# A term of the second layer moved into a PSUM group, and row sums moved from VectorE to ScalarE, in a four-layer graph kernel

## Chip, cores and metric

One core of one Trainium2 chip. The metric is the device time of one execution in microseconds (us). Each kernel is compared with the kernel before on the same chip, in the same rounds. A ratio is the mean time of one kernel's fast runs over that of the other's of the same rounds, so it is not quite the ratio of the medians that I quote; the bracket behind it is its 95% interval. Lower is better.

## The reference

Four graph layers over one 4096 x 4096 weighted adjacency matrix `adj` (f32) and 4096 nodes of 128 features. Each layer is added to its input and normalised. The change touches three of its lines, one in the second layer and two in the last:

```python
# second layer: two Chebyshev convolutions (K = 3)
out = Tx0 @ W[0] + Tx1 @ W[1] + (2.0 * (L @ Tx1) - Tx0) @ W[2] + b     # Tx1 = L @ Tx0, L = adj
# third layer: attention with 4 heads of 32; tau_sum sums over the sources
tau = adj_t * exp(max(0.2 * C, C));  z = (adj_t * tau / tau_sum) @ h_prime
# last layer: mean over the neighbours
deg = clip(sum(adj, axis=1), 1.0);   out = h @ W_self + (adj @ h / deg) @ W_neigh
```

## The kernel before

The second layer makes three products with the adjacency matrix, each as eight blocks of 512 columns, 32 matmuls (4096 rows in tiles of 128) into one PSUM bank per block; each matmul leaves two records in the trace. PSUM is the memory that TensorE adds its products up in; a group is a run of matmuls that add into one bank, and the copy that takes the sum out is called its evacuation. A chunk is the piece of `adj` that a load brings. In what follows "product one" multiplies x, "product two" t1 = adj x, "product three" v = 2 h W2. Product one also sums the degrees, which only the last layer needs:

```python
def propagate(stationary, order=range(NB), look=None):
    for ib in range(NB):
        p = ps_acc.tile([P, IB], F32, name="pacc")
        for n, c in enumerate(order):
            a = chunk(ld, adjT, ib, c)
            if look: look(a, n == 0)
            for k in range(TB):
                nc.tensor.matmul(p, stationary(c * TB + k), a[:, k, :], start=..., stop=...)
        yield ib, slice(ib * IB, (ib + 1) * IB), p

def degree(a, first_one):                       # product one, VectorE, per chunk
    s = l1h.tile([P, 2, IB], F32, name="dhalf")
    nc.vector.tensor_add(s, a[:, 0:2, :], a[:, 2:4, :])
    ...                                         # two more additions into dsum

for ib, blk, p in propagate(lambda jt: x[:, jt, :], finished, degree):
    nc.scalar.copy(t1T[:, blk], p)
    pd = ps_mm.tile([P, TB], F32, name="pmm")
    for k in range(TB):
        nc.tensor.matmul(pd[:, k:k + 1], dsum[:, k * P:(k + 1) * P], ones, start=True, stop=True)
    nc.vector.tensor_scalar_max(rdeg[:, ib * TB:(ib + 1) * TB], pd, 1.0)
    q = transpose4(ps_tr, "ptr", ...)
# ... product two ...
for ib, blk, p in propagate(lambda jt: v[:, jt, :]):            # product three
    nc.scalar.copy(lvT, p)
    for k in range(TB):
        nc.tensor.matmul(q[:, k, :], lvT[...], ident, start=True, stop=False)
        for hh in range(HH):
            nc.tensor.matmul(q[:, k, :], hT[:, hh, ...], W1B[:, HH + hh, :], start=False, stop=...)
    # then ph = h (W0 - W2), two matmuls of 512 columns
```

The third layer runs in eight passes, (mp, hp): four blocks of 1024 columns, two pairs of heads. A pass walks over 32 row tiles. For each, ScalarE squares 704 columns of the chunk, VectorE makes `tau` and part of `tau2`, GpSimd the rest, TensorE sums `den` and `num`. At the end of a pass ScalarE evacuates the sums:

```python
    sq = l2w.tile([P, OWN], F32, name="sq", bufs=2)
    nc.scalar.activation(sq, a[:, 0:OWN], AF.Square)
    ...
# end of a pass
nd = l2w.tile([P, 2, IB], F32, name="nd")
nc.scalar.copy(nd[:, 1, :], den)
nc.scalar.copy(nd[:, 0, :], num)
q = transpose4(ps_x, "px", lambda k: nd[:, 1, k * P:(k + 1) * P])
```

The order of the instructions on each engine is not that of the source: it is chosen at build time, within what the buffers and the data allow.

Of the kernel before, what the change touches and what calls it, by code (L numbers as in the profile page):

```python
# [10 lines left out]
F32 = mybir.dt.float32  # L11
BF16 = mybir.dt.bfloat16
# [20 lines left out]
def adj_resnorm_d4(ctx: ExitStack, tc: tile.TileContext, x_in, xT_in, adj, adjT, w0g, w0gT, a0, w1a, b1a,  # L33
# [53 lines left out]
    mv = const.tile([P, NT, 2], F32, name="mv")  # L87
    es = const.tile([P, NT, H], F32, name="es")
    cs = const.tile([P, NT, H], F32, name="cs")
    flag = const.tile([1, 1], I32, name="flag")  # L90

    def chunk(pool, src, ib, c):
# [318 lines left out]
    def network(usual):  # L411

        with ExitStack() as whole:
# [4 lines left out]
            with ExitStack() as first, ExitStack() as l1h_pool:  # L418
                ps_acc, ps_tr, ps_mm = [first.enter_context(tc.tile_pool(name=n, bufs=2, space=PSUM, reuse_waits="tile"))
                                        for n in ("ps_acc", "ps_tr", "ps_mm")]  # L420
                if not usual:
                    layer0_general(ps_acc, ps_tr, ps_mm)
                    finished = list(range(NB))
                ld = enter(name="ld", bufs=6)
                if usual:
                    finished = layer0(ld, ps_acc, ps_tr, ps_mm)
                dv = state.tile([96, N], BF16, name="dv")
                selD = state.tile([96, H, P], BF16, name="selD")
                l1 = l1_pools.enter_context(tc.tile_pool(name="l1", bufs=1, reuse_waits="tile"))
                l1w = l1_pools.enter_context(tc.tile_pool(name="l1w", bufs=2, reuse_waits="tile"))  # L430
                l1h = l1h_pool.enter_context(tc.tile_pool(name="l1h", bufs=1, reuse_waits="tile"))
                W1A = l1h.tile([P, 3, HID], F32, name="W1A")
                nc.scalar.dma_start(W1A, w1a.rearrange("k p f -> p k f"))
                W1B = l1h.tile([P, 3 * HH, F], F32, name="W1B")
                nc.scalar.dma_start(W1B, w1b.rearrange("k (h p) f -> p (k h) f", p=P))

                def elu(dst, p, bias):
                    r = l1w.tile([P, IB], F32, name="elu_r")
                    n = l1w.tile([P, IB], F32, name="elu_n")
                    nc.scalar.activation(r, p, AF.Relu, bias=bias)  # L440
                    nc.vector.tensor_scalar(n, p, bias, 0.0, op0=ALU.add, op1=ALU.min)
                    nc.scalar.activation(n, n, AF.Exp)
                    nc.vector.scalar_tensor_tensor(dst, n, -1.0, r, op0=ALU.add, op1=ALU.add)

                def propagate(stationary, order=range(NB), look=None):


                    for ib in range(NB):
                        p = ps_acc.tile([P, IB], F32, name="pacc")
                        for n, c in enumerate(order):  # L450
                            a = chunk(ld, adjT, ib, c)
                            if look:
                                look(a, n == 0)
                            for k in range(TB):
                                nc.tensor.matmul(p, stationary(c * TB + k), a[:, k, :], start=n == 0 and k == 0,  # L455
                                                 stop=n == NB - 1 and k == TB - 1)
                        yield ib, slice(ib * IB, (ib + 1) * IB), p

                t1 = state.tile([P, NT, F], F32, name="t1", tag="yn")
                t1T = l1.tile([P, N], F32, name="t1T", tag="t1T")  # L460
                hT = l1h.tile([P, HH, N], F32, name="hT")
                wd = l1h.tile([P, HH, F], F32, name="wd")
                nc.vector.tensor_sub(wd, W1B[:, 0:HH, :], W1B[:, 2 * HH:3 * HH, :])
                w2x = l1h.tile([P, HH, F], F32, name="w2x")
                nc.vector.tensor_scalar_mul(w2x, W1B[:, 2 * HH:3 * HH, :], 2.0)
                dsum = l1h.tile([P, IB], F32, name="dsum")

                def degree(a, first_one):

                    s = l1h.tile([P, 2, IB], F32, name="dhalf")  # L470
                    nc.vector.tensor_add(s, a[:, 0:2, :], a[:, 2:4, :])
                    if first_one:
                        nc.vector.tensor_add(dsum, s[:, 0, :], s[:, 1, :])
                    else:
                        nc.vector.tensor_add(dsum, dsum, s[:, 0, :])
                        nc.vector.tensor_add(dsum, dsum, s[:, 1, :])


                for ib, blk, p in propagate(lambda jt: x[:, jt, :], finished, degree):
                    nc.scalar.copy(t1T[:, blk], p)  # L480
                    pd = ps_mm.tile([P, TB], F32, name="pmm")
                    for k in range(TB):
                        nc.tensor.matmul(pd[:, k:k + 1], dsum[:, k * P:(k + 1) * P], ones, start=True, stop=True)
                    nc.vector.tensor_scalar_max(rdeg[:, ib * TB:(ib + 1) * TB], pd, 1.0)
                    q = transpose4(ps_tr, "ptr", lambda k: t1T[:, (ib * TB + k) * P:(ib * TB + k + 1) * P])
                    nc.vector.tensor_copy(t1[:, ib * TB:(ib + 1) * TB, :], q)
                nc.vector.reciprocal(rdeg, rdeg)

                v = state.tile([P, NT, F], F32, name="v")
                for ib, blk, p in propagate(lambda jt: t1[:, jt, :]):  # L490
                    t2T = l1w.tile([P, IB], F32, name="t2T")
                    nc.vector.scalar_tensor_tensor(t2T, p, 2.0, xT[:, blk], op0=ALU.mult, op1=ALU.subtract)
                    for hh in range(HH):
                        ph = ps_mm.tile([P, IB], F32, name="pmm")
                        for k, r in enumerate((xT[:, blk], t1T[:, blk], t2T)):
                            nc.tensor.matmul(ph, W1A[:, k, hh * P:(hh + 1) * P], r, start=k == 0, stop=k == 2)  # L496
                        elu(hT[:, hh, blk], ph, B1A[:, hh:hh + 1])
                    q = ps_tr.tile([P, TB, F], F32, name="ptr")
                    for k in range(TB):
                        for hh in range(HH):  # L500
                            nc.tensor.matmul(q[:, k, :], hT[:, hh, (ib * TB + k) * P:(ib * TB + k + 1) * P],
                                             w2x[:, hh, :], start=hh == 0, stop=hh == HH - 1)
                    nc.vector.tensor_copy(v[:, ib * TB:(ib + 1) * TB, :], q)


                w = state.tile([P, NT, F], F32, name="w", tag="yn")
                h0T = l1.tile([P, N], F32, name="h0T", tag="t1T")
                for ib, blk, p in propagate(lambda jt: v[:, jt, :]):
                    lvT = l1w.tile([P, IB], F32, name="t2T")
                    nc.scalar.copy(lvT, p)  # L510
                    q = ps_tr.tile([P, TB, F], F32, name="ptr")
                    for k in range(TB):
                        nc.tensor.matmul(q[:, k, :], lvT[:, k * P:(k + 1) * P], ident, start=True, stop=False)
                        for hh in range(HH):
                            nc.tensor.matmul(q[:, k, :], hT[:, hh, (ib * TB + k) * P:(ib * TB + k + 1) * P],  # L515
                                             W1B[:, HH + hh, :], start=False, stop=hh == HH - 1)
                    nc.vector.tensor_copy(w[:, ib * TB:(ib + 1) * TB, :], q)  # L517
                    ph = ps_mm.tile([P, IB], F32, name="pmm")
                    for hh in range(HH):
                        nc.tensor.matmul(ph, wd[:, hh, :], hT[:, hh, blk], start=hh == 0, stop=hh == HH - 1)  # L520
                    nc.scalar.copy(h0T[:, blk], ph)
# [68 lines left out]
            def attention(l2w, bufs, mp, hp):  # L590
# [20 lines left out]
                for nt in range(NT):  # L611
# [4 lines left out]
                    a = a2t[:, nt % 2, :]  # L616
                    sq = l2w.tile([P, OWN], F32, name="sq", bufs=2)
                    nc.scalar.activation(sq, a[:, 0:OWN], AF.Square)  # L618
                    tau = l2w.tile([P, 2, WB], F32, name="tau", bufs=bufs)
                    tau2 = l2w.tile([P, 2, WB], F32, name="tau2", bufs=bufs)  # L620
                    E = lambda h: es[:, nt, 2 * hp + h:2 * hp + h + 1]
# [112 lines left out]
            for mp in range(NW):  # L734
                for hp in range(H // 2):
                    if (mp, hp) != (0, 0):
                        for _ in attention(l2w, 3, mp, hp):
                            next(pieces, None)
                for _ in pieces:
                    pass  # L740
                for j in (2 * mp, 2 * mp + 1):
# [35 lines left out]
```

## Time and profile before

| | before |
|---|---|
| time, median of 3 | 2380.44 us (2375.94 to 2380.57) |
| profiled span | 2376.4 us |
| layer one | 371.7 |
| products one, two, three | 233.4, 274.0, 257.8 |
| last product of layer two with attention pass (0,0) | 347.1 |
| the other seven passes | 108.7, 129.0, 108.2, 119.9, 110.4, 118.4, 110.4 |
| from the last evacuation to the end | 87.3 |

The rows add up to the span. A pass is read as the time from one evacuation of `den` to the next; the seven are (0,1), (1,0), (1,1), (2,0), (2,1), (3,0), (3,1).

### The profile page before, as it was taken

To read this page: it belongs to the slowest core of one execution; us is meant where nothing else is said; L and a number is where in the kernel's file an instruction comes from. 1 tells how busy PE (TensorE), PEld (TensorE's weight loads), DVE (VectorE), ACT (ScalarE), POOL (GpSimd) and SP (SyncE) were. 2 spreads that over 40 slices of the span, in tenths; PEclk is the share of its full clock that TensorE was granted. 3 is DMA by queue.
4 is the path that set the end of the run, shared out by engine and by line. 5 is a ranking of instruction groups with operands and counts; after the bars stand their busy time and mean duration, and the time that the engine had idled before them with its cause. 6 is when DMAs were issued, how large, how long until landed. Compare 5 with 4: busy or idle time off the path is not lost.

```text
span 2376.4 us, 23290 instructions
## 1 busy us (share of the span) xinstructions
PE 2247.5 (95%) x8798; PEld 860.8 (36%) x8798; DVE 1371.0 (58%) x1981; ACT 484.2 (20%) x716; POOL 847.5 (36%) x541
## 2 busy tenths in 40 slices
PE   5899999999999999999999998879998999999988
PEld 3334444444444444444433332112222222222233
DVE  4443458777110110000156656999799999999965
ACT  5665000000000000000122121223222222322220
POOL 0000000000000000000043424999698899889950
PEclk8899999999999999999999998999999999999999
DMA  9988888999878778888877774446665666666655
GB/s 363 347 274 263 246 246 263 290 294 291 263 243 264 233 233 261 280 263 258 262 256 235 266 265 160 146 156 229 213 213 195 209 216 231 212 217 229 220 193 188
DMA packets 261802, 575.39 MB, mean 242 GB/s; under 512 B 9776, under 2 KB 15920, under 8 KB 261680
## 3 DMA queue, kind: packets, MB, share of 16 engines
q1 hardware_dynamic: 252352, 566.27, 73.3%
q10 hardware_dynamic: 9328, 7.54, 1.0%
q8 instruction: 71, 1.16, 0.2%
q14 instruction: 51, 0.42, 0.1%
HBM read 571.67 MB, written 2.10 MB: 241 GB/s over the span
## 4 chain that ended last, share of the span: by engine, by line
PE 83%; DVE 9%; DMA 4%; issue 2%; ACT 1%; POOL 1%; DVEq 0%; ACTq 0%; POOLq 0%
PE pacc L455 27%; PE pacc L319 10%; PE den L607 10%; PE pp L677 10%; PE pp L712 10%; PE num L607 7%; DVE tau L623 5%; DMA chunk<-in_adjT 3%; PE pmm L496 2%; PE num L677 1%; PE px L103 1%; PE pden L305 1%; DVE tau L624 1%; PE ptr L314 1%; PE px L663 1%
## 5 line engine op out<-in xcount | busy, mean ns | idle before, releaser
L623 DVE SCALAR_TENSOR_TENSOR tau<-d,es,chunk 128x1024 f32<-128x1024 f32 x512 | 634.9, 1277 | 25.1 <-issue 16.2
L627 POOL TENSOR_TENSOR tau<-tau,chunk 128x1024 f32<-128x1024 f32 x256 | 611.4, 2388 | 54.8 <-DVE tau L623 47.1
L607 PE MATMUL den<-tau,cs 128*32 128x512 f32 x2048 | 457.5, 605 | 8.6 <-DVE tau L623 8.1
L585 POOL TENSOR_TENSOR x<-x,B2R 128x512 f32<-128x512 f32 x8 | 10.1, 1268 | 1245.1 <-PE px L103 1245.1
L607 PE MATMUL num<-tau,hc 128*32 128x512 f32 x2048 | 413.8, 601 | 32.1 <-POOL tau L627 27.6
L618 ACT ACTIVATE sq<-chunk 128x704 f32<-128x704 f32 x256 | 201.5, 791 | 605.6 <-DVE tau L624 528.9
L626 POOL TENSOR_TENSOR tau<-tau,chunk 128x320 f32<-128x320 f32 x256 | 226.0, 883 | 115.7 <-PE num L607 46.9
L319 PE MATMUL pacc<-chunk,hw 128*128 128x512 f32 x512 | 254.8, 635 | 3.0 <-DVE hw L352 3.0
L677 PE MATMUL pp<-chunk,xT 128*128 128x512 f32 x448 | 243.5, 637 | 11.8 <-DMA chunk<-in_adjT 11.4
L624 DVE SCALAR_TENSOR_TENSOR tau<-d,es,sq 128x704 f32<-128x704 f32 x256 | 241.8, 944 | 18.9 <-PE num L607 14.1
L712 PE MATMUL pp<-chunk,w 128*128 128x512 f32 x512 | 235.6, 602 | 1.2 <-DVE t2T L718 1.2
L455 PE MATMUL pacc<-chunk,x 128*128 128x512 f32 x512 | 223.6, 594 | 0.0
L455 PE MATMUL pacc<-chunk,t 128*128 128x512 f32 x512 | 223.6, 592 | 0.0
L455 PE MATMUL pacc<-chunk,v 128*128 128x512 f32 x512 | 221.4, 592 | 0.0
L607 PEld LDWEIGHTS num<-tau,hc 128*32 128x32 f32 x2048 | 82.2, 109 | 248.2 <-POOL tau L627 83.5
L607 PEld LDWEIGHTS den<-tau,cs 128*32 128x32 f32 x2048 | 86.0, 108 | 222.3 <-issue 106.0
L299 DVE TENSOR_SCALAR pos<-chunk 128x2048 bf16<-128x2048 f32 x92 | 110.8, 1222 | 75.4 <-DMA chunk<-in_adjT 69.6
L517 DVE COPY w<-ptr 128x512 f32<-128x512 f32 x8 | 5.5, 692 | 246.1 <-PE ptr L515 246.1
L455 PEld LDWEIGHTS pacc<-chunk,v 128*128 128x128 f32 x512 | 97.1, 190 | 121.5 <-issue 121.5
L455 PEld LDWEIGHTS pacc<-chunk,t 128*128 128x128 f32 x512 | 96.1, 190 | 114.8 <-issue 114.8
L712 PEld LDWEIGHTS pp<-chunk,w 128*128 128x128 f32 x512 | 92.2, 190 | 124.6 <-issue 117.7
L455 PEld LDWEIGHTS pacc<-chunk,x 128*128 128x128 f32 x512 | 95.8, 190 | 113.4 <-issue 113.4
(171 smaller groups left out, 1461.1 us busy)
## 6 DMA issues: line engine op xcount, KB each, us to landing
chunk<-in_adjT SPq DMA_DIRECT2D x412, 1024.0 KB, 5.5
chunk<-in_adj SPq DMA_DIRECT2D x128, 1024.0 KB, 5.3
xT<-in_xT ACTq DMA_DIRECT2D x8, 256.0 KB, 6.6
out<-o ACTq DMA_DIRECT2D x8, 256.0 KB, 3.6
W1A<-in_w1a ACTq DMA_DIRECT2D x1, 384.0 KB, 3.5
W1B<-in_w1b ACTq DMA_DIRECT2D x1, 384.0 KB, 4.4
W0T<-in_w0gT ACTq DMA_DIRECT2D x1, 64.0 KB, 4.0
W<-in_w0g ACTq DMA_DIRECT2D x1, 64.0 KB, 6.5
```

The costliest lines, as they stand in the source:

```text
L299: nc.vector.tensor_scalar(pos, a, 0.0, None, op0=ALU.is_gt)
L319: nc.tensor.matmul(p, hw[:, j * TB + k, :], a[:, k, :], start=first and k == 0, stop=last and k == TB - 1)
L455: nc.tensor.matmul(p, stationary(c * TB + k), a[:, k, :], start=n == 0 and k == 0, stop=n == NB - 1 and k == TB - 1)
L496: nc.tensor.matmul(ph, W1A[:, k, hh * P:(hh + 1) * P], r, start=k == 0, stop=k == 2)
L607: nc.tensor.matmul(acc[q:q + 32, :], weights(nt, 2 * hp + h, is_den), r[:, h, mb * IB:(mb + 1) * IB], start=nt == 0, stop=nt == NT - 1)
L618: nc.scalar.activation(sq, a[:, 0:OWN], AF.Square)
L623: nc.vector.scalar_tensor_tensor(tau[:, h, :], D[h], E(h), a, op0=ALU.max, op1=ALU.mult)
L624: nc.vector.scalar_tensor_tensor(tau2[:, 0, 0:OWN], D[0][:, 0:OWN], E(0), sq, op0=ALU.max, op1=ALU.mult)
L626: nc.gpsimd.tensor_tensor(tau2[:, 0, OWN:WB], tau[:, 0, OWN:WB], a[:, OWN:WB], ALU.mult)
L627: nc.gpsimd.tensor_tensor(tau2[:, 1, :], tau[:, 1, :], a, ALU.mult)
L677: nc.tensor.matmul(p, y[:, (2 * mp + c) * TB + k, :], a[:, k, :], start=c == 0 and k == 0, stop=c == 1 and k == TB - 1)
L712: nc.tensor.matmul(p, w[:, c * TB + k, :], a[:, k, :], start=c == 0 and k == 0, stop=c == NB - 1 and k == TB - 1)
```

## The change

The intent: take the degree sums off VectorE and TensorE in product one, where TensorE is the bound, and let ScalarE, which has room, take them from the chunks that the third layer loads anyway; and let the term h W1 ride in the open PSUM group of product three in wide matmuls, so that what follows is a plain transpose.

```diff
-                def propagate(stationary, order=range(NB), look=None):
+                def propagate(stationary, order=range(NB), beside=None):
 ...
+                            if beside and n == 0:
+                                beside(p, ib)
 ... (function degree, dsum, the eight blocks' degree matmuls and clips: removed)
+                def times_w1(p, ib):
+                    for hh in range(HH):
+                        nc.tensor.matmul(p, W1B[:, HH + hh, :], hT[:, hh, ib * IB:(ib + 1) * IB], start=False, stop=False)
+                for ib, blk, p in propagate(lambda jt: v[:, jt, :], beside=times_w1):
 ...
-                    for k in range(TB):
-                        nc.tensor.matmul(q[:, k, :], lvT[...], ident, start=True, stop=False)
-                        for hh in range(HH): nc.tensor.matmul(q[:, k, :], hT[...], W1B[:, HH + hh, :], ...)
+                    q = transpose4(ps_tr, "ptr", lambda k: lvT[:, k * P:(k + 1) * P])
 ...                                             # attention, right behind the square
+                    if hp == 0:
+                        junk = l2w.tile([P, WB], BF16, name="junk")
+                        nc.scalar.activation(junk, a, AF.Copy, accum_out=deg[:, nt, mp:mp + 1])
 ...                                             # before the last two layer-three blocks
+                    nc.vector.tensor_reduce(rdeg, deg, AX.X, ALU.add)      # then max 1.0, reciprocal
```

More of the change, by code (lines that the diff above doesn't have):

```diff
@@ L89, in adj_resnorm_d4 @@
     cs = const.tile([P, NT, H], F32, name="cs")
+    deg = const.tile([P, NT, NW], F32, name="deg")
     flag = const.tile([1, 1], I32, name="flag")
@@ L451, in propagate @@
                             a = chunk(ld, adjT, ib, c)
-                            if look:
-                                look(a, n == 0)
                             for k in range(TB):
@@ L465, in network @@
                 nc.vector.tensor_scalar_mul(w2x, W1B[:, 2 * HH:3 * HH, :], 2.0)
-                dsum = l1h.tile([P, IB], F32, name="dsum")
-                def degree(a, first_one):
-                    s = l1h.tile([P, 2, IB], F32, name="dhalf")
-                    nc.vector.tensor_add(s, a[:, 0:2, :], a[:, 2:4, :])
-                    if first_one:
-                        nc.vector.tensor_add(dsum, s[:, 0, :], s[:, 1, :])
-                    else:
-                        nc.vector.tensor_add(dsum, dsum, s[:, 0, :])
-                        nc.vector.tensor_add(dsum, dsum, s[:, 1, :])
-                for ib, blk, p in propagate(lambda jt: x[:, jt, :], finished, degree):
+                for ib, blk, p in propagate(lambda jt: x[:, jt, :], finished):
                     nc.scalar.copy(t1T[:, blk], p)
-                    pd = ps_mm.tile([P, TB], F32, name="pmm")
-                    for k in range(TB):
-                        nc.tensor.matmul(pd[:, k:k + 1], dsum[:, k * P:(k + 1) * P], ones, start=True, stop=True)
-                    nc.vector.tensor_scalar_max(rdeg[:, ib * TB:(ib + 1) * TB], pd, 1.0)
                     q = transpose4(ps_tr, "ptr", lambda k: t1T[:, (ib * TB + k) * P:(ib * TB + k + 1) * P])
                     nc.vector.tensor_copy(t1[:, ib * TB:(ib + 1) * TB, :], q)
-                nc.vector.reciprocal(rdeg, rdeg)
                 v = state.tile([P, NT, F], F32, name="v")
@@ L507, in network @@
                 h0T = l1.tile([P, N], F32, name="h0T", tag="t1T")
-                for ib, blk, p in propagate(lambda jt: v[:, jt, :]):
+                def times_w1(p, ib):
+                    for hh in range(HH):
+                        nc.tensor.matmul(p, W1B[:, HH + hh, :], hT[:, hh, ib * IB:(ib + 1) * IB], start=False, stop=False)
+                for ib, blk, p in propagate(lambda jt: v[:, jt, :], beside=times_w1):
                     lvT = l1w.tile([P, IB], F32, name="t2T")
                     nc.scalar.copy(lvT, p)
-                    q = ps_tr.tile([P, TB, F], F32, name="ptr")
-                    for k in range(TB):
-                        nc.tensor.matmul(q[:, k, :], lvT[:, k * P:(k + 1) * P], ident, start=True, stop=False)
-                        for hh in range(HH):
-                            nc.tensor.matmul(q[:, k, :], hT[:, hh, (ib * TB + k) * P:(ib * TB + k + 1) * P],
-                                             W1B[:, HH + hh, :], start=False, stop=hh == HH - 1)
+                    q = transpose4(ps_tr, "ptr", lambda k: lvT[:, k * P:(k + 1) * P])
                     nc.vector.tensor_copy(w[:, ib * TB:(ib + 1) * TB, :], q)
@@ L738, in network @@
                             next(pieces, None)
+                if mp == NW - 1:
+                    nc.vector.tensor_reduce(rdeg, deg, AX.X, ALU.add)
+                    nc.vector.tensor_scalar_max(rdeg, rdeg, 1.0)
+                    nc.vector.reciprocal(rdeg, rdeg)
                 for _ in pieces:
```

## The prediction

> **What bounds the kernel now.** I read the page first, then the chain of work that ended last, then the busy time of each engine in windows cut at the stage borders, then the lines and timelines of the parts that the change touches.
>
> ```profile
> PE 2247.5 (95%) x8798; PEld 860.8 (36%) x8798; DVE 1371.0 (58%) x1981; ACT 484.2 (20%) x716; POOL 847.5 (36%) x541
> ...
> PE 83%; DVE 9%; DMA 4%; issue 2%; ACT 1%; POOL 1%; DVEq 0%; ACTq 0%; POOLq 0%
> ```
>
> TensorE is busy 95% of the span and is 83% of the chain; ScalarE is busy 20% and is 1% of the chain. By these two lines work taken from TensorE counts, work taken from VectorE hardly does, and ScalarE has room. An average over stages can mislead, so the stages:
>
> ```profile
> core 0: us, PE busy (x) PEld busy (x) DVE busy (x) ACT busy (x) POOL busy (x), PEclk, DMA share, GB/s
> 371.80:606.70 234.90, 233.95 (x631) 110.01 (x632) 174.25 (x254) 6.27 (x12) 0.00 (x0) 1.00 0.92 290
> ...
> 909.00:1137.00 228.00, 228.00 (x674) 111.97 (x673) 5.54 (x8) 8.37 (x15) 0.00 (x0) 1.00 0.84 264
> ...
> 1961.00:2073.00 112.00, 106.25 (x588) 26.63 (x587) 108.96 (x123) 28.86 (x41) 103.23 (x66) 1.00 0.65 226
> 2073.00:2190.00 117.00, 115.70 (x617) 31.80 (x616) 110.44 (x105) 30.91 (x48) 105.27 (x68) 1.00 0.64 216
> ```
>
> 371.8 to 606.7 is the second layer's first product, where the degrees are summed now; 909 to 1137 most of its third product. In both TensorE is busy for the whole window, but for 0.95 us in the first. VectorE's 174 us beside it lie under TensorE. The last two windows are the third layer's attention, one pass of 32 row tiles each (2073 to 2190 is one that will get the degree sums, 1961 to 2073 one that will not). There VectorE, TensorE and GpSimd are all nearly full, and ScalarE is at a quarter. So the saving, if any, is in the first two stages and the risk in the attention.
>
> What stands between the products now:
>
> ```profile
> 402.65 1.05 PE L483 MATMUL pmm<-ones,dsum 128*128 128x1 f32 x8 [0.95 <-DVE dsum L476]
> 403.56 1.10 PE L455 MATMUL pacc<-chunk,x 128*128 128x512 f32 x2
> 404.50 0.60 PE L103 MATMUL ptr<-ident,t1T 128*128 128x128 f32 x4
> 404.94 7.46 PE L455 MATMUL pacc<-chunk,x 128*128 128x512 f32 x17
> ```
>
> This is TensorE's timeline at the end of the first of eight blocks of product one. The eight records of the degree matmuls hold it from 402.65 to 403.56, after 0.95 us of waiting for VectorE's sum. The four transposes take some 0.43 us.
>
> ```profile
> 433.90 26.61 PE pacc L455 x62
> 462.70 26.61 PE pacc L455 x62
> ...
> 944.96 27.47 PE pacc L455 x64
> 976.97 27.47 PE pacc L455 x64
> ```
>
> From the chain of waits in order of time: blocks of the first product follow each other every 28.80 us, those of the third every 32.01 us. A record of a full product matmul takes 26.61/62 = 0.429 us, and each matmul leaves two.
>
> **What the Trainium skill says.** (1) "TensorE: Matmul & The Clock Gate", Back-to-back issue gap, gives N/2.4 + 2.5 ns for one isolated warm matmul, 216 ns for N=512. The trace has 0.858 us for a matmul here (f32, two records), four times that; I use the trace. (2) "ScalarE: Activation LUTs", What ACT_TABLE_LOAD costs: 186 ns + 0.833 ns per element for an ACTIVATE without pointer operands, 1039 ns at N=1024. The trace's nearest is the summing pass of layer one, 1913 ns for 2048 elements (the formula gives 1892), so it agrees within 2%, but it is followed by a read of the accumulator of 191 ns, which counts too. (3) Table sets on that page says that copy is in every set as filler; so the new copies should load no table, and the built programs do have equally many loads. No run shows it yet. (4) "PSUM — Partial Sum Buffer", The four PSUM rules: a matmul without the first flag adds where the bit is set, so two more matmuls inside an open group need no extra wait or evacuation. The trace agrees so far as the 64 records of a group run at 0.429 us each with no idle time.
>
> **The change part by part.** The built programs differ by these counts, half of each being in a fallback branch that does not run: 32 one-column matmuls less; 64 matmuls of 128 columns (W1B under hT) replaced by 16 of 512 columns; 32 products with the identity become transposes; 184 additions and 8 clips less on VectorE; 128 summing copies more on ScalarE; three small VectorE operations more.
>
> 1. First product. Per block the degree matmuls cost 403.56 - 402.65 = 0.91 us, so 8 x 0.91 = 7.3 us, plus the one wait of 0.95 us: 8.2 us, all on the path. The new period should be 64 x 0.429 + 0.43 = 27.9 us.
>
> 2. Third product. The period of 32.01 us less 64 x 0.429 = 27.47 leaves 4.54. Four records of the wd product are 4 x 0.429 = 1.72, which leaves 2.82 for the 24 records of the old mix of identity and W1B (8 + 16), 0.1175 each. After: two wide matmuls are four records, 1.72 us, and four transposes, one record each, 0.43 (as in the first product) to 0.58 (as in the last layer's): 2.15 to 2.30. Gain 0.52 to 0.67 per block, 4.2 to 5.4 in eight. The arithmetic of the W1 term is the same before and after; the gain is only that narrow f32 matmuls are dear (0.1175 us for 128 columns against 0.107 for a quarter of a wide one) and that a transpose is one record instead of two.
>
> 3. VectorE, first product:
>
> ```profile
> L471 DVE TENSOR_TENSOR dhalf<-chunk 128x1024 f32<-128x1024 f32 x64 | 78.4, 1224 | 2.0
> ...
> L476 DVE TENSOR_TENSOR dsum<-dsum,dhalf 128x512 f32<-128x512 f32 x56 | 38.7, 692 | 1.8
> L475 DVE TENSOR_TENSOR dsum<-dsum,dhalf 128x512 f32<-128x512 f32 x56 | 38.7, 691 | 1.6
> ```
>
> With 5.5 us of first additions 161 us of VectorE go, 93% of its work in that window. Beyond the 0.95 us they are worth nothing, since TensorE had no other wait on them.
>
> 4. ScalarE, attention. A summing copy of 1024 is 1913 - 1024 x 0.833 = 1060 ns, with the read 1.25 us; 128 of them are 160 us, 40 in each of the four passes over the first pair of heads. ScalarE goes from 31 to some 71 of 117 us: it does not become the bound by its sum. The squares (L618, 791 ns) are what VectorE needs from it, and they run two row tiles ahead, since they have two buffers.
>
> 5. End: three operations on 128x32 values, under 1 us (an estimate from the 353 ns of the reciprocal of that size), in the 2.5 us in which VectorE waits for the denominators' transposes before L639. Nothing.
>
> Sum on TensorE: 8.2 + 4.8 = 13 us.
>
> **Where ScalarE can give it back.** ScalarE runs in program order, so a copy whose chunk has not landed holds the squares behind it. In the comparison of the two orders the copies come in pairs ahead of squares of earlier tiles: in the third pass for instance the copies of tiles 26 and 27 stand before the square of tile 23. I took each chunk's landing from the trace of before, added 2.5 us for the pair and 0.8 us for the square, and compared with the time at which VectorE started on that square. Of 128 copies nearly all leave 0.5 to 10 us; the worst are -0.8 us in pass (1,0), -1.8 in (2,0), and -1.7 and -1.9 before and in (3,0). So some 6 us in all if each is paid in full, and the later part of a pass may not pay since a delay already there covers the next. One place shows what it looks like:
>
> ```profile
> 1649.99 0.59 ACT L684 COPY acc<-pp 128x512 f32<-128x512 f32 x1 [7.98 <-PE pp L677]
> 1650.48 1.47 ACT L618 ACTIVATE sq<-chunk 128x704 f32<-128x704 f32 x2
> 1651.31 0.95 DVE L624 SCALAR_TENSOR_TENSOR tau<-d,es,sq 128x704 f32<-128x704 f32 x1 [1.25 <-ACT sq L618]
> ```
>
> ScalarE waited 8 us for a product, two squares were late, and VectorE lost 1.25 us. Pass (1,0) has four such places. I take 5 us for ScalarE in all.
>
> **The rivals.** (a) ScalarE costs nothing: the copies fall into its idle time (its squares sat 495 us waiting for VectorE in the attention). For it: the busy sums and most of the margins. Then 2378 - 13 = 2365. (b) ScalarE's order becomes the wait: margins of 0.5 to 3 us go too, since chunks land later as passes shift, and the layer-three blocks' short chain of ScalarE copies gets copies of 1.25 us ahead of them. For it: only 4 chunks or so stand between landing and use in the later passes. That would give back 10 to 18 us: 2375 to 2383, a wash. (c) The relief of VectorE frees chunks earlier and the loads start earlier. DMA is at 0.92 of its time in that window, but TensorE has no wait on a load there: nothing. (d) The first product was bound by VectorE at block ends oftener than once; then the gain would be over 8.2 us. Against it: the idle time before the degree matmuls is 0.95 us in all.
>
> **Range and chances.** The three times lie from 2375.9 to 2380.6, so I start from 2378 rather than the median. 2378 - 13 + 5 = 2370. Rival (a) is the low side, (b) the high side, with some 4 us for the changed order in the attention on each side: 2361 to 2381. Faster by over 2% (under 2333) would need 47 us, more than three times what TensorE loses of work: 0.01. Slower by over 2% (over 2428) would need ScalarE to cost 60 us, some half microsecond in each of the 128 tiles: 0.02. Within 2%: 0.97.
>
> **What would show it.** Right: blocks of product one every 27.9 us, of product three every 31.3 to 31.5 us, TensorE without idle time in both; 128 summing copies of 1.06 us with a read of 0.19 us each; 20 table loads as now; attention passes over the first heads longer by 0 to 3 us each, with VectorE's waits for the squares up from 2.7 us to 5 or 8. Wrong: the third product's period staying near 32 (wide matmuls or transposes dearer than taken); the passes with copies longer by over 5 us, with ScalarE waiting for chunks in front of the copies (rival b); or passes shorter than now, which nothing here explains.

## The result, and the profile after

The changed kernel is correct and takes 2375.57 us (median of 4, 2370.89 to 2377.05) against 2379.89 us (median of 4): ratio 0.9982 [0.9964, 1.0]. It lies in the range that was predicted and in "within 2%", but the forecast gain of some 8 to 10 us came out as 4.3, with an interval that just reaches no gain. In five further rounds the same kernel gave 2374.3 us and 0.9977 [0.9965, 0.999]. Some 5 us of 13 are left.

The changed kernel's page, busy time and chain:

```profile
PE 2241.0 (94%) x8606; PEld 841.0 (35%) x8606; DVE 1209.7 (51%) x1791; ACT 618.9 (26%) x972; POOL 847.5 (36%) x541
...
PE 82%; DVE 8%; DMA 5%; issue 2%; ACT 2%; POOL 1%; DVEq 0%; ACTq 0%; POOLq 0%
```

VectorE lost 161 us of work and ScalarE gained 135, and the end hardly moved: neither was the bound. ScalarE's share of the chain rose from 1% to 2% and that of DMA from 4% to 5%, which is a first hint. The chain in order of time (start us, us, what), in products one and three:

```profile
430.94 27.47 PE pacc L454 x64
...
458.88 11.16 PE pacc L454 x26
...
907.78 1.72 PE pacc L495 x4
909.49 24.03 PE pacc L454 x56
933.52 0.86 PE pmm L504 x2
934.38 0.47 PE ptr L104 x4
...
939.15 1.72 PE pacc L495 x4
```

Product one's blocks now follow every 458.88 - 430.94 = 27.94 us (28.80 before), product three's every 939.15 - 907.78 = 31.37 us (32.01 before). The two wide W1 matmuls are four records and 1.72 us, the four transposes 0.47 us. Both gains came as worked out: the ledger has product one at 225.8 (-7.6) and product three at 253.3 (-4.5). The loss is in the attention. The seven passes took 819.7 us against 805.0 in this execution, 14.7 more, and 814.0 in the profiled execution of the second batch, 9.0 more.

What stands there is read best at the end of pass (2,1). ScalarE's timeline of the kernel before at that place (in brackets: idle before, and what ended it):

```profile
2056.71 0.79 ACT L618 ACTIVATE sq<-chunk 128x704 f32<-128x704 f32 x1 [3.01 <-DVE tau L624]
2060.30 0.59 ACT L635 COPY nd<-den 128x512 f32<-128x512 f32 x1 [2.80 <-PE den L607]
```

ScalarE waits for `den` and evacuates it at once. The same place in the changed kernel:

```profile
2041.47 1.46 ACT L602 ACTIVATE sq<-chunk 128x704 f32<-128x704 f32 x2
2049.08 1.06 ACT L605 ACTIVATE junk<-chunk 128x1024 bf16<-128x1024 f32 x1 [6.15 <-DMA chunk<-in_adj]
...
2051.32 0.77 ACT L602 ACTIVATE sq<-chunk 128x704 f32<-128x704 f32 x1
2051.99 1.04 ACT L605 ACTIVATE junk<-chunk 128x1024 bf16<-128x1024 f32 x1
...
2053.16 1.06 ACT L605 ACTIVATE junk<-chunk 128x1024 bf16<-128x1024 f32 x1
...
2054.89 0.56 ACT L622 COPY nd<-den 128x512 f32<-128x512 f32 x1
```

ScalarE stands 6.15 us in front of a summing copy of the *next* pass, because its chunk has not landed. Behind it in ScalarE's order are the squares of this pass and the evacuation of `den`. TensorE, changed kernel:

```profile
2051.84 0.60 PE L581 MATMUL d<-dv,selD 96*128 96x512 bf16 x2
2055.51 0.69 PE L104 MATMUL px<-ident,nd 128*128 128x128 f32 x2 [3.06 <-ACT nd L622]
```

TensorE's last records of `den` end at 2051.92 (a group of six from 2050.47, 1.45 us), so the evacuation came about 3 us late and TensorE waited 3.06 us for it. In those 3 us ScalarE was not waiting: it made the last two of four summing copies, and a square, that had piled up behind the late chunk. Six copies of the next pass stand ahead of the evacuation at the ends of (0,1) and (1,1) as well; there their chunks landed early enough, and the evacuation begins within 0.1 us of the last `den` record, as in the kernel before. Behind the wait TensorE's granted clock fell (the share of its full clock that the profile shows as granted); the windows of the changed kernel (columns as in the prediction's table; the granted clock is the third figure from the right):

```profile
2050.00:2055.00 5.00, 2.45 (x18) 0.50 (x14) 3.46 (x4) 4.94 (x11) 3.20 (x3) 0.96 0.89 306
2055.00:2058.00 3.00, 2.49 (x11) 0.50 (x11) 0.00 (x0) 1.15 (x2) 2.29 (x1) 0.50 0.79 307
2058.00:2061.00 3.00, 2.48 (x16) 1.49 (x16) 1.68 (x3) 1.63 (x3) 0.06 (x1) 0.50 0.00 0
...
2065.00:2070.00 5.00, 4.17 (x17) 1.55 (x18) 5.00 (x7) 3.64 (x10) 3.23 (x2) 1.00 0.00 0
```

For about ten microseconds TensorE ran at half clock. It is tempting to add that to the cost, but degonly, a kernel told of below, has the same order of instructions from pass (2,0) on and much the same wait, with the clock at 1.00 behind it:

```profile
2059.86 0.44 PE L104 MATMUL px<-ident,nd 128*128 128x128 f32 x2 [3.29 <-ACT nd L623]
```

```profile
2055.00:2060.00 5.00, 1.71 (x11) 0.38 (x8) 2.74 (x3) 4.97 (x10) 3.01 (x2) 1.00 0.86 275
2060.00:2065.00 5.00, 3.86 (x30) 1.23 (x34) 3.00 (x4) 2.32 (x5) 3.15 (x3) 1.00 0.37 150
```

Its clock fell only behind a later wait, at 2068 us and for about 3 us. Its passes (2,1) and (3,0) took 113.5 and 121.7 us, the changed kernel's 113.3 and 121.7. So the longer stretch of half clock cost nothing here that the passes show. The Trainium skill, "TensorE: Matmul & The Clock Gate", What's actually happening, says that the clock gate halves the array's clock after an idle window of about 3.4 us, with a window that runs freely. The traces agree only in part: 3.06 us of waiting were followed by 0.50 here, and 3.29 us in degonly were not.

### The profile page after: what moved, and what is told of

It reads as the page before. It is cut to its first block, busy times and chain, and to the rows that moved or that the text cites. A ratio compares the mean times of both kernels' runs of the same rounds, so it can differ in the third digit from the quotient of the medians.

```text
span 2375.2 us, 22876 instructions
## 1 busy us (share of the span) xinstructions
PE 2241.0 (94%) x8606; PEld 841.0 (35%) x8606; DVE 1209.7 (51%) x1791; ACT 618.9 (26%) x972; POOL 847.5 (36%) x541
## 3 DMA queue, kind: packets, MB, share of 16 engines
q8 instruction: 69, 1.13, 0.2%
## 4 chain that ended last, share of the span: by engine, by line
PE 82%; DVE 8%; DMA 5%; issue 2%; ACT 2%; POOL 1%; DVEq 0%; ACTq 0%; POOLq 0%
PE pacc L454 28%; PE pacc L320 10%; PE pp L699 10%; PE pp L664 9%; PE den L591 9%; PE num L591 7%; DVE tau L610 5%; DMA chunk<-in_adjT 3%; PE pmm L480 2%; PE px L104 1%; PE num L664 1%; DVE tau L611 1%; PE pden L306 1%; DMA chunk<-in_adj 1%; PE px L650 1%
## 5 line engine op out<-in xcount | busy, mean ns | idle before, releaser
L591 PE MATMUL den<-tau,cs 128*32 128x512 f32 x2048 | 464.3, 609 | 11.9 <-DVE tau L610 11.5
L591 PE MATMUL num<-tau,hc 128*32 128x512 f32 x2048 | 420.0, 605 | 33.5 <-POOL tau L614 26.8
L569 POOL TENSOR_TENSOR x<-x,B2R 128x512 f32<-128x512 f32 x8 | 10.1, 1267 | 1228.4 <-PE px L104 1228.4
L605 ACT ACTIVATE junk<-chunk 128x1024 bf16<-128x1024 f32 x128 | 134.9, 1054 | 111.0 <-DMA chunk<-in_adj 105.2
L454 PEld LDWEIGHTS pacc<-chunk,v 128*128 128x128 f32 x512 | 97.3, 190 | 121.9 <-issue 121.9
```

Of the source, the lines that this page charges most:

```text
L591: nc.tensor.matmul(acc[q:q + 32, :], weights(nt, 2 * hp + h, is_den), r[:, h, mb * IB:(mb + 1) * IB], start=nt == 0, stop=nt == NT - 1)
L605: nc.scalar.activation(junk, a, AF.Copy, accum_out=deg[:, nt, mp:mp + 1])
```

## The experiments

Ten kernels were run, all with five rounds. Theory A: the built order put most of the copies 2 to 8 row tiles ahead of the squares, and a copy whose chunk has not landed holds the squares and evacuations behind it. Rival B: ScalarE's 160 us (the sum of the copies' and reads' records; since records overlap, its busy time rose by 135) themselves are too much, wherever they stand; B': they are too dense in the passes that have them.

**nocopy: no degree work at all (result wrong, relative error 0.207).**

```diff
-                    if hp == 0: junk = ...; nc.scalar.activation(junk, a, AF.Copy, accum_out=...)
-                    nc.vector.tensor_reduce(rdeg, deg, AX.X, ALU.add) ...
+                    nc.vector.memset(rdeg, 0.125)
```

> The change with no degree work at all (rdeg is a constant, so the result is wrong on purpose). Its TensorE order from layer two's last product on is that of the kernel before, in every pass. All theories: the two products gain what they gained in the changed kernel, 8.1 + 4.6 = 12.7 us, so -12.7 us against before (-11 to -14). If it gains less than 9 us, the loss of the attention passes is not due to the copies at all.

Measured: 2367.87 us, 0.9952 [0.9938, 0.9966]; seven passes 804.5. Without the copies the passes are those of before. So the whole loss comes with the copies, and some 6.5 us are there to be had beyond the changed kernel's 2374.3.

**bound: the same copies, each right behind its own square.** The copy writes behind the square in one tile, so a copy cannot be ordered ahead of the squares before it. Correct. In the built program all 128 copies follow their own square, where the changed kernel has them up to 8 tiles ahead.

```diff
-                    sq = l2w.tile([P, OWN], F32, name="sq", bufs=2)
+                    sqj = l2w.tile([P, OWN + WB // 2], F32, name="sq", bufs=2)
+                    sq = sqj[:, 0:OWN]
-                        junk = l2w.tile([P, WB], BF16, name="junk")
+                        junk = sqj[:, OWN:OWN + WB // 2].bitcast(BF16)
```

> The whole change, but each summing copy writes its unused output into the same double buffer as its tile's square, so that it can't be ordered ahead of that square: in the built program each copy stands right behind its own square. The result is right. Theory A (the copies are ordered 2 to 8 tiles ahead of the squares, ScalarE then waits for chunks that have not landed and holds the squares and evacuations behind them): the 14.8 us given back in the passes from (1,0) on come back but for 0 to 3 us, so -10 to -13 us against before, ScalarE's waits of copies for chunks under 10 us (97.7 in the changed kernel). Rival B (the 160 us of ScalarE time themselves delay squares and evacuations, wherever they stand): it still gives back 10 to 15 us, so +2 to -3 us against before.

Measured: 2368.11 us, 0.9953 [0.994, 0.9966], as fast as having no copies. ScalarE does the same work in another order (the build moved some instructions of TensorE and VectorE too, see "What stays open"). Bound, ScalarE, end of pass (2,1):

```profile
2047.36 0.79 ACT L603 ACTIVATE sq<-chunk 128x704 f32<-128x704 f32 x1 [3.02 <-DVE tau L612]
2048.06 1.04 ACT L606 ACTIVATE sq<-chunk 128x1024 bf16<-128x1024 f32 x1
...
2050.95 0.58 ACT L623 COPY nd<-den 128x512 f32<-128x512 f32 x1 [1.76 <-PE den L591]
```

The evacuation again waits for `den`, not for a chunk (the second line is the summing copy, under the name of the shared tile). This is what theory A says of the pass end, and no copy waited for a chunk any more. But the seven passes still took 812.3 us in the profiled execution, 7.3 over before where 0 to 3 were forecast; 5.1 of these are in passes (1,0) and (1,1), of which more below.

**short: copies of 64 columns at the changed kernel's places (wrong, relative error 0.652).**

```diff
-                        nc.scalar.activation(junk, a, AF.Copy, accum_out=...)         # junk [P, WB]
+                        nc.scalar.activation(junk, a[:, 0:64], AF.Copy, accum_out=...) # junk [P, 64]
```

> The whole change, but each summing copy reads only 64 of the 1024 columns (wrong result on purpose), in the same places of ScalarE's order as in the changed kernel: the same waits for chunks, a quarter of the time. Theory A: the waits for chunks stay (60 to 100 us) and most of the loss with them, so 5 to 11 us given back of the 12.7, -2 to -8 us against before. Rival B: the loss goes with the length of the copies, -11 to -13 us.

Measured: 2368.8 us, 0.9952 [0.9938, 0.9966]; seven passes 812.4. ScalarE's order is nearly unchanged, each copy is short, and most of the loss of time is gone: 10.7 us under before by the medians, near what rival B forecast (-11 to -13 us) and not theory A (-2 to -8). So the place alone is not the whole cause either; place and length together are. The end of pass (2,1) shows how:

```profile
2045.73 0.26 ACT L605 ACTIVATE junk<-chunk 128x64 bf16<-128x64 f32 x1 [7.05 <-DMA chunk<-in_adj]
...
2049.61 0.56 ACT L622 COPY nd<-den 128x512 f32<-128x512 f32 x1
```

ScalarE waits as long for the same chunk, but reaches the evacuation 3.9 us after it landed, where the changed kernel needs 5.8; TensorE waits 1.21 us for it instead of 3.06.

**w1only: the W1 half of the change alone** (the kernel before with `beside` and the plain transposes; degrees as before). Correct.

> Only the first half of the change: W1 in the third product's group and plain transposes; the degrees stay with VectorE and TensorE. The orders of VectorE and TensorE in the attention are those of the kernel before. All theories: blocks of the third product every 31.43 us instead of 32.01, -4.6 us against before (-3 to -6), attention passes as before.

Measured: 2372.69 us, 0.9974 [0.9962, 0.9987]; product one 233.4, product three 253.3, seven passes 804.0. The W1 half is worth its 4.5 us in product three and leaves the passes alone. Timed, the medians differ by 6.8 us, somewhat over the forecast 3 to 6; the interval covers both.

**after_again: the changed kernel, in the second batch.**

> The changed kernel once more, with more rounds and beside the next three on one chip. All theories: as in its first runs, -3 to -6 us against before; its attention passes from (0,1) to (3,1) sum to 819.7 us within 1 us (805.0 before), since the passes have repeated to 0.5 us between kernels where nothing was changed.

Measured: 2374.3 us, 0.9977 [0.9965, 0.999]. Its seven passes took 814.0 us, so the forecast (819.7 within 1 us) was missed, and this shows what in the ledger is luck. Pass (1,1) took 112.3 us in the first profile and 108.3 in this one, with the same instructions in the same order. TensorE, first profile and second:

```profile
1734.21 2.08 PE L664 MATMUL pp<-chunk,xT 128*128 128x512 f32 x2 [2.57 <-DMA chunk<-in_adjT]
```

```profile
1731.99 1.13 PE L664 MATMUL pp<-chunk,xT 128*128 128x512 f32 x2 [1.17 <-DMA chunk<-in_adjT]
```

A load came 1.4 us later in one execution; behind the longer wait the clock of the window 1735 to 1740 is 0.50 in the first and 1.00 in the second, and the same two matmuls take 2.08 us instead of 1.13. Pass (1,1) took 108.1 to 108.9 us in all seven executions in which its granted clock was 1.00, and 109.9 to 112.3 in the five with 0.97 or 0.98 (before and ten experiments' profiles and the first of the changed kernel). Pass (1,0) varies as well (131.6 and 129.2 us in the two executions). So passes (1,0) and (1,1) are not used to tell kernels apart. Passes (2,0), (2,1) and (3,0) repeat within 0.7 us in sum between the two executions, and they are.

**degonly: the degree half alone** (the changed kernel with product three as before). Correct.

> Only the second half of the change: the degrees by ScalarE, the third product as before. The orders of TensorE, VectorE and ScalarE in the attention are those of the changed kernel. First product 225.8 us (-7.6); passes 819 to 820, 14 to 15 us more than before; the first pass some 2 us less by its order. Theory A and B alike: -1 to +6 us against before, a wash by itself.

Measured: 2381.51 us, 1.0008 [0.9995, 1.0022]; product one 225.8, product three 257.8. The degree half alone is a wash: what product one gains, the attention gives back (seven passes 817.3, where 819 to 820 were forecast).

**split: bound, with the copies spread over both passes of a block.** Correct.

```diff
-                    if hp == 0:
+                    if hp == nt % 2:
```

> The copies bound to their squares as in the run called bound, but those of even tiles in the pass over the first pair of heads and of odd tiles in that over the second, so every pass has 16 instead of 32 or none. Theory A (order is what costs): about as bound, -10 to -13 us; what bound still loses in the passes (7.3 us over the kernel before, 812.3 against 805.0) may fall to 3 to 7. Rival B' (what is left of the loss is the density of ScalarE work within a pass): 2 to 4 us better than bound, the passes with few copies unchanged and the passes (2,0) and (3,0) back near 119.9 and 118.4.

Measured: 2368.07 us, 0.9952 [0.9939, 0.9965], the same as bound; but passes (2,0), (2,1), (3,0) took 346.8 us, less than before.

**bound15: bound with half as much copying again** (a second copy of 512 columns behind the first). Correct.

```diff
+                        nc.scalar.activation(junk[:, 0:IB], a[:, 0:IB], AF.Copy, accum_out=deg2[:, nt, mp:mp + 1])
```

> The kernel called bound with a second copy of half a tile behind each copy (its sum isn't used; the result is right): 1.25 + 0.8 us instead of 1.25 per tile, so some 66 us of copies in a pass of about 120 and ScalarE at nearly 100 of 120. Theory A (the length of the copies does not matter as long as they stand behind their squares): within 3 us of bound, -8 to -12 us against before, passes (2,0) and (3,0) within 1 us of 121.0 and 119.5. Rival B (ScalarE's time delays squares): the 7.3 us that bound lost grow by half or more, passes (2,0) and (3,0) each 2 us or more longer than in bound.

Measured: 2371.02 us, 0.9963 [0.9949, 0.9977], 2.9 us over bound, though the two intervals overlap. Pass (2,0) took 122.4 us, 1.4 over bound's, and (3,0) the same 119.5: between the forecasts of A (within 1 us) and B (2 us or more in each). In these passes the other engines have the very order of bound, so the 1.4 us go with ScalarE's work, unless they are chance: the granted clock of that pass was 0.97 against 0.99. That more copying costs something even in the good order is likely, not shown.

By then it was open where in a pass the places do harm: at its end, as in the timeline above (theory C), or all along it (rival D). Two kernels share the copies out between the two orders. Each is bound with one more condition, and both are correct.

```diff
-                        junk = sqj[:, OWN:OWN + WB // 2].bitcast(BF16)
+                        if nt < 8:                        # tailfree;  nt >= 8 in tailheld
+                            junk = sqj[:, OWN:OWN + WB // 2].bitcast(BF16)
+                        else:
+                            junk = l2w.tile([P, WB], BF16, name="junk")
```

In the built tailfree one copy of the next pass stands ahead of the evacuation that ends pass (2,1), as in bound, with the later copies up to 6 tiles ahead of the squares. In tailheld six stand ahead of it, as in the changed kernel, and the copies of tiles 9 to 32 are bound.

**tailfree**

> Correct. The copies of the first eight row tiles of each pass stand behind their own squares, so none stands ahead of the copies that evacuate the pass before; those of tiles 9 to 32 keep the lead of 1 to 6 tiles that they have in the changed kernel. Measure: passes (2,0), (2,1) and (3,0) together, 348.7 us before, 357.8 and 357.5 in two executions of the changed kernel, 350.9 with all copies bound. Theory C (the loss sits at the pass ends: six copies of the next pass hold the evacuation, TensorE waits 3 us for it and its clock is halved behind the wait): pass (2,1) back to 110.4, pass (3,0) 119 to 120, the three together 350 to 353, no wait of TensorE for the evacuation, time about 2369. Rival D (the loss is made in the body of the passes, where copies stand ahead of squares): the three together still 355 to 358, time about 2374.

Measured: 2371.27 us, 0.9965 [0.9952, 0.9979]; passes 122.2, 110.4, 121.6, together 354.2. TensorE at the end of pass (2,1):

```profile
2049.33 0.60 PE L581 MATMUL d<-dv,selD 96*128 96x512 bf16 x2
2050.08 0.44 PE L104 MATMUL px<-ident,nd 128*128 128x128 f32 x2
```

**tailheld**

> Correct. The opposite half: only the copies of the first eight row tiles keep their lead, so that six of them stand ahead of the evacuation at the end of passes (0,1), (1,1) and (2,1) as in the changed kernel; all others are bound behind their own squares. Theory C: pass (2,1) stays near 113.4, pass (3,0) at 121 to 122, the three together 355 to 357, TensorE waits some 3 us for the evacuation once and the granted clock falls to 0.5 behind it; time about 2373. Rival D: the three together 350 to 352 as with all copies bound, time about 2368.

Measured: 2372.73 us, 0.9969 [0.9956, 0.9983]; passes 120.7, 113.3, 120.7, together 354.7. TensorE at the same place:

```profile
2048.22 0.60 PE L581 MATMUL d<-dv,selD 96*128 96x512 bf16 x2
2051.88 0.44 PE L104 MATMUL px<-ident,nd 128*128 128x128 f32 x2 [3.06 <-ACT nd L626]
```

(In the expectation of tailfree 357.8 for the first execution of the changed kernel was a slip; its three passes add up to 356.8.) The wait of 3.06 us and the extra 3 us of pass (2,1) are there with the six copies ahead and gone without: that part of theory C is shown. Its other part, that the halved clock costs time, is not; degonly speaks against it. But tailfree keeps more than C allowed, and tailheld less. Both are half right, as the table shows.

| kernel | (2,0) | (2,1) | (3,0) | sum | over before |
|---|---|---|---|---|---|
| before, nocopy, w1only | 119.9 | 110.4 | 118.4 | 348.7 | 0 |
| split | 118.2 | 110.4 | 118.2 | 346.8 | -1.9 |
| bound | 121.0 | 110.4 | 119.5 | 350.9 | 2.2 |
| bound15 | 122.4 | 110.4 | 119.5 | 352.3 | 3.6 |
| short | 120.8 | 111.5 | 120.6 | 352.9 | 4.2 |
| tailfree | 122.2 | 110.4 | 121.6 | 354.2 | 5.5 |
| tailheld | 120.7 | 113.3 | 120.7 | 354.7 | 6.0 |
| changed kernel | 121.8 | 113.3 | 121.7 | 356.8 | 8.1 |
| the same again | 122.1 | 113.5 | 121.9 | 357.5 | 8.8 |
| degonly | 122.3 | 113.5 | 121.7 | 357.5 | 8.8 |

Over bound, the leads along the pass cost 5.5 - 2.2 = 3.3 us (tailfree) and the six copies at its end 6.0 - 2.2 = 3.8 us (tailheld). Together with bound's own 2.2 that is 9.3, against 8.1 to 8.8 measured for all of it: the parts add up within 0.5 to 1.2 us. Bound's own 2.2 us fits rival B', since the same copies at half the density cost nothing (split). All rows but the first and the changed kernel's rest on one profiled execution each. Rival B in its plain form falls: the same 160 us of work cost 8.8 or 2.2 or nothing, depending on where they stand.

## Why the prediction was right or wrong

1. *Product one, 8.2 us.* Right: 7.6, period 27.94 where 27.9 was expected.
2. *Product three, 4.2 to 5.4 us.* Right: 4.5, alone (w1only) as in the whole change. W1's four records took 1.72 us as used, the four transposes 0.47 where 0.43 to 0.58 was taken.
3. *VectorE's 161 us are worth nothing.* Right, so far as runs show it: product one gained no more than TensorE's own share, and TensorE has no wait left there but one of 0.2 us.
4. *ScalarE, "I take 5 us for ScalarE in all".* **This is the step that failed.** It was the only term of the sum with a plus sign. The durations in it were right (copies 1054 ns in the mean, reads of the accumulator 188 ns, 20 table loads before and after), though ScalarE's busy time rose by 135 us and not 160, because records overlap. So was the mechanism, a chunk that has not landed. Its size was 8.1 to 8.8 us in the three passes that repeat, and 14.7 in all seven in the first profile, of which 6.4 in passes (1,0) and (1,1) (243.9 against 237.5 us) did not repeat in the second, where the granted clock was 1.00 instead of 0.97. Two things were missing in the working:
   - The margins were taken for squares only. The evacuation at the end of a pass stands behind six copies of the next pass as well, and TensorE, not VectorE, waits for it: 3.06 us at the end of (2,1), the one of three such ends where the chunk was late; 3.8 us in the three passes (tailheld over bound). The prediction allowed the passes *with* copies 0 to 3 us each; it had nothing for pass (2,1), which has none and became 3.0 us longer.
   - A delayed square was charged once, as its negative margin. In the seven passes VectorE's waits for squares rose from 2.7 us in 4 places to 10.1 in 10, where 5 or 8 us were expected, and the leads along the pass cost 3.3 us in three passes (tailfree over bound), with 3.4 us of such waits there and none in bound. They are not the whole cost: short lost 4.2 us in these passes with 0.4 us of such waits.
   Rival (b) said just this, "ScalarE's order becomes the wait", and priced it at 10 to 18 us; it deserved more than the upper edge of the range.
5. *The end: nothing.* Right as far as it can be told: the tail was 88.2 and 88.1 us against 87.3, and 86.5 to 88.4 over all profiles.

Not in any step: the stretch of the last layer-two product with pass (0,0) was 4.1 us shorter in the first profile and 2.4 in the second. It ranged from 343.0 to 347.1 us over all profiles, and no part of the change accounts for it; I leave it open. The terms that repeat, -7.6 - 4.5 + 8.1 to 8.8, give -3.3 to -4.0 us; timed, the medians differ by -4.3 and -5.1.

**What stays open.** The order of TensorE's instructions in passes (1,0), (2,0) and (3,0) differs too between the changed kernel, bound and before, because the build orders all engines together; I could not fix one engine's order alone, so a part of the 3.3 us may be TensorE's. Short has TensorE's order of before in all passes but (1,0), and its three passes still lost 4.2 us, so ScalarE's order does cost by itself. Of these 4.2 us 1.1 are the pass end shown above; the rest is not traced further.

The best version is bound or split, correct and at 2368 us: 0.5% under before, and about 6 us under the change as it was made. As fast as having no degree work at all, within the interval of some 3 us.

## What to carry to other kernels

Work given to an engine with much idle time is free only in the right places of its program order: look at what stands *behind* each added instruction, evacuations included, and whether the added one can be waiting for data that nothing else behind it needs. Where the data come early enough, as at two of the three pass ends here, the same order costs nothing. If the build may hoist it, tie it to the instruction that it should follow, for instance by letting both write one buffer. And test a two-part change in halves: here one half was worth all of the gain that was kept.

## What the Trainium skill lacked or had wrong

- "ScalarE: Activation LUTs", What ACT_TABLE_LOAD costs: its 186 ns + 0.833 ns per element gives 1039 ns for a copy of 1024 elements, and the trace has 1039 to 1077. What it lacks is the read of the accumulator behind each summing copy, an instruction of its own of 188 ns in the mean. ScalarE's busy time rose by 134.7 us for 128 copies and reads, 1.05 us for a pair: as the records overlap, the pair adds no more than the copy's record alone.
- "TensorE: Matmul & The Clock Gate", What's actually happening: the half clock is told for idle windows of about 3.4 us. Here it came behind single waits of 3.06 us (0.50 for ten microseconds) and of 2.57 us (0.50 over 1735 to 1740), and not behind one of 1.17 us nor one of 3.29 us (degonly). So the length of a single wait did not decide it. What the half clock costs is open too: pass (1,1) was 4.0 us longer with a wait that was 1.4 us longer, passes (2,1) and (3,0) no longer than without it.
- "PSUM — Partial Sum Buffer", Engine vs sequencer instructions, does say that ScalarE's queue is strictly first in, first out, and the trace agrees: nothing passed the copy that waited 6.15 us. What no page that I used puts a price on is the order that the build chooses within it: 3.8 us at the pass ends alone (tailheld against bound).
